# A cross-attention kernel: two TensorE products placed behind their neighbours

## The chip, the cores and the metric

The kernel runs on one core of a Trainium2 chip. A core has TensorE (PE: matrix products, with its weight loads shown apart as PEld), VectorE (DVE), ScalarE (ACT), GpSimd (POOL) and SyncE (SP), and 16 DMA engines. The metric is the time of one execution on the device, in microseconds (us). All data are float32.

## The reference

Thirty-two batches b, each with x and y of 256 channels x 1024 positions:

```python
x_q = einsum('oc,bcn->bno', w_qk, y)
x_k = einsum('oc,bcn->bon', w_qk, x)
x_v = einsum('oc,bcn->bon', w_v, x) + b_v
energy = einsum('bnc,bcm->bnm', x_q, x_k)
attention = softmax(energy, axis=-1)
attention = attention / (1e-07 + attention.sum(axis=1, keepdims=True))
x_r = einsum('bcn,bnm->bcm', x_v, attention)
x_r = relu(einsum('oc,bcn->bon', w_t, x - x_r) + b_t)
return x + x_r
```

So each batch has an energy of 1024 x 1024, a softmax over its rows, a division by its column sums, and a product with the values, followed by a projection, a Relu and a residual.

## The kernel before, in words

**Algebra.** The two uses of `w_qk` are folded into one 256 x 256 matrix, so that a batch has a product "keys" (class `Keys`, tiles `gx`), and the energy is a product of these with y. The value weights and the last projection are folded as well (class `Values`, tiles `ut`), so that the projected result is one accumulation of an x term and an attention term.

**Seven products.** Each of the four matrix products of a batch (keys, values, energy, attention) is cut into 2 x 2 blocks and made from seven products instead of eight, called p1 to p7, in the manner of Strassen and Winograd. They need sums of blocks of both operands (`xs`, `ys`, `gt`, `us`, `et`), and sums of the seven products give the four output blocks (methods `c11`, `c12`, `c21`, `c22`). The seven products of one instance share three PSUM banks of 128 x 512: `one` takes P1, then P6 is added onto it, then P7, then P4; `two` takes P5, then P3 is added; `three` takes P2. Between the additions, ScalarE copies the bank's state to SBUF: `p1s` behind P1, `w` behind P6, `p5s` behind P5. So P6 may not be added to `one` before `p1s` is copied, P7 not before `w`, P3 not before `p5s`, and P4 not before c22 has read `one`. In the profile a copy's name has the class's letter in front: `op5s` is the copy of P5 in the attention (o), `ew` the copy of P6 in the energy (e). PSUM tiles are `po`, `pe`, `pg`, `pu`.

**Energy.** Rows are taken in four pairs t = 0 to 3 (loop at L603), an `Energy` object each. A product of a pair is one 128 x 128 weight block and 512 columns, which TensorE runs as two passes. Combining the blocks on VectorE also finds the row's minimum or maximum for the softmax (rows with `nm`). P4 of a pair is run in the next pair (L632), between that pair's P6 and P3.

**Attention.** One `Attention` object a batch. Each of its products has an x part (`xpart`, L461: one product with the projection weights, two passes) and an e part (`epart`, L466: four row tiles, eight passes). The e operands are the normalised attention and mixes of it that VectorE makes: `et` has t1, t2 and t4. `run` is one hand-written order of all engines' work. While a batch's attention runs, the values of the next batch are finished (`u.p4()` is one of its products, eight passes of 128 columns). The attention's last product P4 (`end()`) and its last output block (`before.c21()`) are done in the next batch's first pair.

**Order.** Every engine but SP is wrapped in `InOrder` (L66): an instruction may not be issued before the one that the program wrote before it on that engine. The order in the text is thus the order on the engine. Most instructions are therefore recorded at L77. DMAs: x, y and the sums' raw blocks are loaded on SP (L95, L236, L237), sums are added by accumulating DMAs issued on POOL (L110), and outputs are stored on SP (L483).

The places of the change: in `run`, the lines L515 to L520; in the main loop, L610 to L628.

Of the kernel before, what the change touches and what calls it, by code (L numbers as in the profile page):

```python
# [16 lines left out]
def kernel(  # L17
# [30 lines left out]
    B, C, N = x.shape  # L48
# [40 lines left out]
    def load(tag, b, pieces=1):  # L89
        from_, p = (x, xp) if tag == "x" else (y, yp)  # L90
        to = p.tile([P, KC, N], F32, tag=tag, name=f"{tag}_{b}")
        from_ = from_[b].rearrange("(k p) n -> p k n", p=P)
        W = KC // pieces
        for j in range(pieces):
            nc.sync.dma_start(to[:, ts(j, W)], from_[:, ts(j, W)])  # L95
        loaded[tag, b] = to
# [121 lines left out]
    def summed(tag, b):  # L218


        p = up if tag == "x" else one
        s = p.tile([P, 4, MB], F32, tag=f"{tag}s", name=f"{tag}s_{b}")
        t1, t3, t4, t2 = (s[:, j] for j in range(4))
        to = loaded[tag, b]
        b11, b12 = to[:, 0, ts(0, MB)], to[:, 0, ts(1, MB)]
        b21, b22 = to[:, 1, ts(0, MB)], to[:, 1, ts(1, MB)]
        if b == 0:
            pool.tensor_tensor(t1, b11, b12, ALU.add)
            pool.tensor_tensor(t2, b22, t1, ALU.add)
            pool.tensor_tensor(t3, b12, b22, ALU.add)  # L230
            pool.tensor_tensor(t4, b21, t2, ALU.add)
            steps = []
        else:
            from_ = (x if tag == "x" else y)[b]
            q = quarters(from_)
            nc.sync.dma_start(s[:, :2], q[:, 0, 1:2, :].to_broadcast([P, 2, MB]))  # L236
            nc.sync.dma_start(s[:, 2:], q[:, 1])  # L237
            steps = [
                lambda: accumulate(s[:, :2], corners(from_)),
                lambda: accumulate(s[:, 2:], s[:, 0:1].to_broadcast([P, 2, MB])),  # L240
                lambda: accumulate(t4, q[:, 1, 1]),
            ]
        return (b11, b21, b22, t4, t1, t2, t3), steps
# [191 lines left out]
    class Attention(Seven):  # L435
# [69 lines left out]
        def run(self, u):  # L505

            self.normal(0, 0)
            if u:
                u.c22()
            self.normal(1, 0)  # L510
            self.normal(0, 1)
            self.mix(self.t1, self.b11, self.b12, ALU.add)
            self.normal(1, 1)
            self.mix(self.t2, self.t1, self.b22, ALU.subtract)
            self.epart(self.one, 1)  # L515
            self.p1s = self.biased(self.one, "p1s", bt[:, 0, :])
            self.epart(self.three, 2)
            self.xpart(self.one, 6, True)
            self.epart(self.two, 5)
            self.p5s = self.biased(self.two, "p5s", bt[:, 1, :])  # L520
            if u:
                u.p4()
                u.c21()
                u.c11()
                u.c12()
            self.c11()
            self.xpart(self.two, 3, True)
            self.epart(self.two, 3, range(HT // 2))
            self.epart(self.one, 6)
            self.w = self.biased(self.one, "w", nbt[:, 0, :])  # L530
            self.mix(self.t3, self.b12, self.b22, ALU.subtract)
            self.mix(self.t4, self.b21, self.t2, ALU.subtract)
            self.epart(self.two, 3, range(HT // 2, HT))
            self.c12()
            self.xpart(self.one, 7, True)
            self.epart(self.one, 7)
            self.c22()
# [5 lines left out]
    def columns(b):  # L543

        part = one.tile([P, NB], F32, tag="part", name=f"part_{b}")
        dve.tensor_reduce(
            part, acc.rearrange("p (j r) -> p j r", r=G32), AX.X, ALU.add, apply_transpose=True
        )
        return part

    def inverse(b, part):

        pS = bank(f"pS_{b}")
        pe.matmul(pS[:, :NB], fold.rearrange("p a c -> p (a c)"), part, start=True, stop=True)
        sc = one.tile([P, NB, 1], F32, tag="sc", name=f"sc_{b}")
        dve.tensor_scalar(sc[:, :, 0], pS[:, :NB], EPS, None, ALU.add)
        dve.reciprocal(sc[:, :, 0], sc[:, :, 0])
        rc = one.tile([P, NB, G32], F32, tag="rc", name=f"rc_{b}")
        dve.transpose(rc.rearrange("p j r -> p (j r)"), sc.to_broadcast([P, NB, G32]))
        return rc.rearrange("p j r -> p (j r)")  # L560
# [37 lines left out]
    before = None  # L598
    for b in range(B):
        more = b + 1 < B  # L600
        pair = []

        for t in range(HT):  # L603
            now = Energy(b, t, lhs, rhs)
            pair.append(now)
            now.p1()
            if t > 0:
                pair[t - 1].exp(1)
            now.p5()
            if t == 0:  # L610
                if before is not None:
                    before.end()
                e = ep.tile([P, NT, N], F32, tag="e", name=f"e_{b}")
                acc = one.tile([P, N], F32, tag="acc", name=f"acc_{b}")
                ur, usteps = u.factors()
            if t > 1:
                pair[t - 2].share(0)
            now.p2()
            now.c11()
            if t == 0 and before is not None:  # L620
                before.c21()
                if b + 1 < B:
                    load("x", b + 1)
            if t == 1:
                pair[0].scale(1)
            if t > 1:
                pair[t - 1].share(1)
            now.p6()  # L628
            if t == 1:
                act.activation(acc, e[:, HT, :], AF.Copy, scale=scales[HT])  # L630
            if t > 0:
                pair[t - 1].p4()  # L632
                pair[t - 1].c21()
                pair[t - 1].exp(0)
            now.p3()
            now.c12()
            now.p7()
            now.c22()
            if t == 0:
                for step in usteps:  # L640
                    step()
                if more:
                    xn, xsteps = summed("x", b + 1)
            elif more:
                xsteps[t - 1]()
        last = pair[-1]

        if more:
            g = Keys(b + 1, xn)
            g.p1()  # L650
        last.exp(1)
        if more:
            g.p5()
        pair[2].share(0)
        last.p4()
        last.c21()
        last.share(1)
        if more:
            load("y", b + 1)
            rhs, ysteps = summed("y", b + 1)  # L660
            g.p6()
        last.exp(0)
        if more:
            g.p2()
            g.c11()
            g.p3()
        last.share(0)
        part = columns(b)
        if more:
            g.p7()  # L670
            g.c12()
            g.c22()
            un = Values(b + 1, xn)
            un.p1()
            un.p5()
            un.p2()
            un.p6()
        else:
            now = Attention(b, xr, ur)
            now.begin()  # L680
        rc = inverse(b, part)
        if more:
            un.p3()
            g.p4()
            g.c21()
            un.p7()
            lhs, gsteps = g.factors()

        if more:
            now = Attention(b, xr, ur)  # L690
            now.begin()
            ysteps[0]()
            now.run(un)
            ysteps[1]()
            un.bias()
            for step in gsteps:
                step()
            ysteps[2]()
            before = now
            xr, u = xn, un  # L700
        else:
            now.run(None)
            now.end()
            now.c21()
# [30 lines left out]
```

## Time and profile before

| What | Value |
|---|---|
| median of three runs | 2175.99 us (2175.93 to 2176.82) |
| the profiled execution | 2176.29 us |
| its span, from the first to the last instruction | 2174.5 us |
| mean granted TensorE clock | 0.997 |
| VectorE busy | 83% |
| ScalarE busy | 36% |
| GpSimd busy | 27% |
| HBM traffic over the span | 99 GB/s |
| one 512-wide pass of TensorE, start to start (16 passes `po<-e,ut` from 470.84 to 477.71) | 0.429 us |
| one batch, from the attention's first pass to the next batch's (468.43 to 535.27 in the chain of waits) | 66.84 us |

The profile is one execution, in which the hardware profiler notes each instruction's start and end. A line of its time line gives start, length, engine, source line, operation, output<-inputs, shapes and count; in square brackets stand the idle time of the engine before it and what ended that. Consecutive instructions of a kind are merged, and the length is then from the first start to the last end. Ends of matmuls are modelled: a matmul's row overlaps the next one, so the distance between starts says more than the length. The chain of waits follows the work back from the last instruction, at each step to what released it, and gives each piece's start and length.

TensorE's waits that the profile shows as idle time are few: 4.5 us at the first batch's end for the DMA `xs<-xs`, 2.7 twice in the last batch, and some below 1.5 us.

### The profile page before, as it was taken

How to read it: one execution, taken by the hardware profiler on the slowest of the kernel's cores; microseconds unless marked ns; L12 is line 12 of the kernel's file. 1: busy time of each engine (PE TensorE's matmuls, PEld its weight loads, DVE VectorE, ACT ScalarE, POOL GpSimd, SP SyncE). 2: the span in 40 equal slices, each digit the busy share in tenths (PEclk: the TensorE clock that was granted, in tenths of full speed). 3: DMA queues.
4: the chain of work that ended last, by engine and by line, in shares of the span. 5: the costliest groups of instructions: out<-in, count | busy, mean ns of one | idle time of the engine just before them, and what ended most of it. 6: DMA issues, size and time to landing. Idle time of an engine off the chain costs nothing.

```text
span 2174.5 us, 19911 instructions
## 1 busy us (share of the span) xinstructions
PE 2154.4 (99%) x6366; PEld 1065.1 (49%) x6366; DVE 1803.9 (83%) x2963; ACT 788.3 (36%) x1321; POOL 597.9 (27%) x488
## 2 busy tenths in 40 slices
PE   8999999999999999999999999999999999999997
PEld 4455445554445545455544555444554545554453
DVE  5798888888888988889888889888898888988887
ACT  4234432344432344333443224443234433344421
POOL 4322323222233223232232322223322323223220
PEclk9999999999999999999999999999999999999999
DMA  5555666556655556565566654665555566546630
GB/s 149 128 115 131 152 139 140 117 120 150 151 126 123 122 142 145 126 147 109 131 155 141 135 121 119 149 149 121 129 123 140 145 127 149 111 126 155 145 74 20
DMA packets 139049, 282.60 MB, mean 130 GB/s; under 512 B 9152, under 2 KB 42688, under 8 KB 138944
## 3 DMA queue, kind: packets, MB, share of 16 engines
q0 software_dynamic: 75936, 114.83, 33.9%
q1 hardware_dynamic: 62464, 166.48, 21.4%
q8 instruction: 51, 0.84, 0.2%
q14 instruction: 54, 0.44, 0.1%
q10 hardware_dynamic: 544, 0.00, 0.0%
HBM read 181.67 MB, written 33.55 MB: 99 GB/s over the span
## 4 chain that ended last, share of the span: by engine, by line
PE 97%; DVE 1%; DMA 1%; POOL 0%; issue 0%; ACT 0%; DVEq 0%
PE po L77 44%; PE pe L77 34%; PE pu L77 9%; PE pg L77 9%; DVE e L77 1%; DMA ut<-uc 0%; DMA xs<-xs 0%; DMA xs<-in_x_dram 0%; POOL us L77 0%; DVE acc L77 0%; PE pS L77 0%; PE idle L142 0%; DVE et L77 0%; PE pw L184 0%; PE pg L169 0%
## 5 line engine op out<-in xcount | busy, mean ns | idle before, releaser
L77 PE MATMUL pe<-gt,ys 128*128 128x512 f32 x768 | 394.9, 596 | 0.0
L77 DVE SCALAR_TENSOR_TENSOR e<-e,ri,rc 128x512 f32<-128x512 f32 x512 | 348.4, 742 | 1.1
L77 DVE SCALAR_TENSOR_TENSOR acc<-e,ri,acc 128x1024 f32<-128x1024 f32 x224 | 287.9, 1285 | 8.0
L77 DVE CUSTOM_DVE_ANT_0 e<-pe,ep1s 128x512 f32<-128x512 f32 x128 | 88.5, 691 | 230.2 <-PE pe L77 161.8
L77 PE MATMUL pe<-gx,y 128*128 128x512 f32 x512 | 261.4, 592 | 0.0
L77 PEld LDWEIGHTS pe<-gt,ys 128*128 128x128 f32 x768 | 143.3, 190 | 189.0 <-issue 168.1
L77 PE MATMUL po<-e,us 128*128 128x512 f32 x512 | 235.4, 592 | 0.0
L77 POOL TENSOR_TENSOR gt<-gx 128x512 f32<-128x512 f32 x64 | 101.7, 1589 | 478.4 <-DVE gx L77 478.4
L77 PE MATMUL po<-et,us 128*128 128x512 f32 x512 | 230.2, 592 | 0.0
L77 PE MATMUL po<-e,ut 128*128 128x512 f32 x512 | 226.9, 596 | 2.7 <-DVE e L77 2.7
L77 ACT ACTIVATE e<-e,nm 128x1024 f32<-128x1024 f32 x128 | 147.1, 1149 | 97.6 <-DVE nm L77 96.2
L77 DVE TENSOR_TENSOR e<-e 128x1024 f32<-128x1024 f32 x64 | 178.9, 2833 | 0.0
L77 ACT COPY ep1s<-pe 128x512 f32<-128x512 f32 x128 | 75.0, 586 | 281.5 <-PE pe L77 277.0
L77 PEld LDWEIGHTS po<-e,ut 128*128 128x128 f32 x512 | 98.0, 192 | 126.0 <-issue 94.8
L77 PEld LDWEIGHTS po<-et,us 128*128 128x128 f32 x512 | 97.3, 190 | 122.5 <-issue 121.5
L77 PEld LDWEIGHTS po<-e,us 128*128 128x128 f32 x512 | 97.3, 190 | 122.5 <-issue 115.3
L77 PEld LDWEIGHTS pe<-gx,y 128*128 128x128 f32 x512 | 97.2, 190 | 122.0 <-issue 121.5
L77 ACT ACTIVATE e<-e,bias 128x1024 f32<-128x1024 f32 x128 | 147.4, 1152 | 0.6 <-DVE ri L77 0.5
L77 POOL DMA_DIRECT2D ut<-uc x32 | 50.7, 1584 | 314.2 <-DVE ut L77 259.0
L77 PE MATMUL pe<-gx,ys 128*128 128x512 f32 x256 | 130.8, 592 | 1.1 <-DVE nm L77 1.1
L77 PE MATMUL pe<-gt,y 128*128 128x512 f32 x256 | 130.7, 592 | 0.0
L77 POOL TENSOR_TENSOR us<-ut 128x512 f32<-128x512 f32 x64 | 82.1, 1283 | 165.0 <-PE po L77 147.8
(113 smaller groups left out, 3303.4 us busy)
## 6 DMA issues: line engine op xcount, KB each, us to landing
y<-in_ctx_dram SPq DMA_DIRECT2D x32, 1024.0 KB, 4.9
ut<-uc POOLq DMA_DIRECT2D x32, 1024.0 KB, 9.7
out_dram<-z SPq DMA_DIRECT2D x128, 256.0 KB, 2.1
x<-in_x_dram SPq DMA_DIRECT2D x31, 1024.0 KB, 7.6
xs<-in_x_dram SPq DMA_DIRECT2D x62, 512.0 KB, 4.5
ys<-in_ctx_dram SPq DMA_DIRECT2D x62, 512.0 KB, 4.2
xs<-in_x_dram POOLq DMA_DIRECT2D x31, 512.0 KB, 6.8
xs<-xs POOLq DMA_DIRECT2D x31, 512.0 KB, 5.0
```

The costliest lines, as they stand in the source:

```text
L77: self.last = getattr(self.engine, name)(*args, **kwargs)
```

## The change

Two products change their places in TensorE's order. In the attention, the x part of P6 is issued behind P5's e part and its copy rather than ahead of P5's e part. In the first energy pair of a batch (t = 0), P6 is issued ahead of P2. To keep the program's order consistent with that, the last output block of the batch before (`before.c21()`) and the load of x for the next batch are written ahead of these two products as well. In pairs 1 to 3 the order stays. What is computed stays the same.

```diff
             self.p1s = self.biased(self.one, "p1s", bt[:, 0, :])
             self.epart(self.three, 2)
-            self.xpart(self.one, 6, True)
             self.epart(self.two, 5)
             self.p5s = self.biased(self.two, "p5s", bt[:, 1, :])
+            self.xpart(self.one, 6, True)
             if u:
                 u.p4()
                 u.c21()
...
             if t == 0:
                 if before is not None:
                     before.end()
+                    before.c21()
+                    if more:
+                        load("x", b + 1)
...
             if t > 1:
                 pair[t - 2].share(0)
+            if t == 0:
+                now.p6()
             now.p2()
             now.c11()
-            if t == 0 and before is not None:
-                before.c21()
-                if b + 1 < B:
-                    load("x", b + 1)
             if t == 1:
                 pair[0].scale(1)
             if t > 1:
                 pair[t - 1].share(1)
-            now.p6()
+            if t > 0:
+                now.p6()
```

In TensorE's order, the attention goes from "P1 e, P2 e, P6 x, P5 e, u.p4, P3 x" to "P1 e, P2 e, P5 e, P6 x, u.p4, P3 x". The first pair goes from "P1, P5, end(), P2, P6, P3, P7" to "P1, P5, end(), P6, P2, P3, P7". On VectorE the last addition of `before.c21()` comes ahead of c11 of the first pair. ScalarE's, GpSimd's and SP's orders are the same as before.

## The prediction

> **What bounds the kernel now.** I read the page's busy shares first, then the chain of waits, then the time lines around the two places that the diff touches. The page:
>
> ```profile
> PE 2154.4 (99%) x6366; PEld 1065.1 (49%) x6366; DVE 1803.9 (83%) x2963; ACT 788.3 (36%) x1321; POOL 597.9 (27%) x488
> ```
>
> TensorE is busy nearly all the time, so most of its time is work that this change keeps. Only its waits can be saved, and most of these are too short to stand as idle time: the busy row of a matmul that started late is simply longer. So I count distances between starts. Sixteen passes `po<-e,ut` run from 470.84 to 477.71, which is 0.4294 us a pass; a 512-wide product is two passes, 0.86 us. A product of the values is eight 128-wide passes: 528.67 to 529.56, 0.89 us. Now the chain of one batch (start, length, engine, tile, count):
>
> ```profile
> 535.27 13.73 PE po L77 x32
> 549.01 0.89 PE pu L77 x8
> 549.90 12.22 PE po L77 x28
> ...
> 568.13 21.54 PE pe L77 x50
> ```
>
> All of it is TensorE. 32 passes take what they should (13.74). But 28 passes should take 12.02 and take 12.22, and 50 should take 21.47 and take 21.54. A batch (66.85 us) thus loses about 0.2 us behind `u.p4` and 0.07 in the energy. The time line of the first place:
>
> ```profile
> 549.10 0.69 ACT L77 ACTIVATE op5s<-po,bt 128x512 f32<-128x512 f32 x1 [7.03 <-PE po L77]
> 549.84 0.30 PEld L77 LDWEIGHTS po<-x,wtTs 128*128 128x128 f32 x2
> 549.84 1.12 PE L77 MATMUL po<-x,wtTs 128*128 128x512 f32 x2
> ```
>
> ScalarE's copy of P5 ends at 549.79; the x part of P3, which adds onto the same bank, loads its weights 0.05 us later, and its two loads stand together, so the first pass begins at 549.94. `u.p4` had ended its eight passes at 548.85 + 0.89 = 549.74. Loss 0.20 us. The second place, in the first energy pair:
>
> ```profile
> 502.84 1.02 PE L77 MATMUL pe<-gt,y 128*128 128x512 f32 x2
> 503.04 0.59 ACT L77 COPY ew<-pe 128x512 f32<-128x512 f32 x1 [1.03 <-PE pe L77]
> 503.67 0.30 PEld L77 LDWEIGHTS pe<-gt,ys 128*128 128x128 f32 x2 [0.65 <-ACT ew L77]
> 503.70 1.10 PE L77 MATMUL pe<-gt,ys 128*128 128x512 f32 x2
> 504.64 1.02 PE L77 MATMUL pe<-gx,y 128*128 128x512 f32 x2
> ```
>
> Row 1 is P3, row 4 P7, which adds onto the bank that `ew` copies. 502.84 to 504.64 is 1.80 us where two products take 1.72: loss 0.08 us. In later pairs P4 of the pair before stands between P6 and P3, so the copy is hidden.
>
> **The change part by part.** No instruction is added or removed; a few stand elsewhere.
>
> *P6's x part behind P5.* It moves from before P5's four e tiles to behind them, so P5 and its copy end 0.86 us earlier while `u.p4` and the x part of P3 keep their places. The copy would end at 549.79 - 0.86 = 548.93; the x part of P3 wants its weights at about 549.63. The wait goes: 0.20 us in batches 0 to 30. The moved x part itself waits for `op1s`, which begins at 541.38 and takes 0.69: long done. In batch 25 the same distance holds 0.28 us more (the row at 1753.35 shows 0.21 idle for `op5s`); that goes too. In the last batch there is no `u.p4` between:
>
> ```profile
> 2147.76 3.60 PE L77 MATMUL po<-et,us 128*128 128x512 f32 x8
> 2152.14 1.13 PE L77 MATMUL po<-x,wtTs 128*128 128x512 f32 x2 [0.78 <-ACT op5s L77]
> 2153.10 1.88 PE L77 MATMUL po<-e,us 128*128 128x512 f32 x4
> ```
>
> From 2147.76 eight passes and a product would end at 2152.05, not 2153.10: loss 1.05. With 0.86 us of other work put in between, 0.19 remains: gain 0.86. What follows there isn't bound by VectorE (it idles 1.90 and 2.82 us before its next outputs), so the gain arrives at the end. Part sum: 30 x 0.20 + 0.48 + 0.86 = 7.3 us.
>
> *The cover that is lost.* P5's e tiles now begin 0.86 us earlier, and their operand is t1, which VectorE has only just made:
>
> ```profile
> 543.09 2.34 DVE L77 TENSOR_TENSOR et<-e 128x1024 f32<-128x1024 f32 x2
> ...
> 544.55 1.02 PE L77 MATMUL po<-xs,wtTs 128*128 128x512 f32 x2
> ```
>
> Each half of t1 takes 1.21 us (group mean 1211 ns). Half one is ready at 544.30 and P5 now wants to begin at 544.55: 0.25 us. Half two is ready at 545.43 for a pass at 546.27: far enough. How long from VectorE's end to the first pass? The two waits above give 0.05 to the load and 0.10 more to the pass, 0.15. But P5's first tile waits for two engines (t1 from VectorE, `us` from POOL), and its t1 wait stands as an own instruction in TensorE's queue. The nearest row for that is `pg<-xs,gs` in the opening: `gs` ends at 8.59 (8.30 + 0.29), the loads come at 8.70, the first pass at 8.81: 0.22 us. Ends: 0.15 gives no wait; half as much again as 0.22, 0.33, would be late by 0.08. I take 0.22, the same kind of wait: no stall, but only 0.03 us to spare. The far end gives back 31 x 0.08 = 2.5 us. All that TensorE has to do stands behind this wait, so nothing else would fill it.
>
> *P6 ahead of P2 in pair 0.* P6 now begins at 501.12, where P2 stood. What it waits for is old by then: `ep1s`, the copy of its own bank (496.21 + 0.59), and a sum of y that POOL's `ys<-ys` makes. That is issued once a batch, 27 us before (540.83 for the P6 near 568), and the like transfer `xs<-xs` lands 5.0 us after issue. `ew` comes at 502.18 instead of 503.04, behind the Relu of `c21` on ScalarE (501.32 + 0.69 = 502.01), and ends at 502.77; P7 wants its weights at 503.27. The wait goes: 0.08 us. In batch 0 it buys nothing, since TensorE then stands 4.55 us for the DMA `xs<-xs`. 31 x 0.08 = 2.5 us. P2 is 0.86 us later, and its c11 on VectorE with it: from 502.29 to 503.15, done by 503.84, and VectorE's next (c12) begins at 504.00. The last addition of `before.c21`, which stood behind c11, now goes ahead of it, at about 502.05; what is queued behind it is c11, which comes later anyway. So the store and the load of x on SP leave about 0.85 us earlier (503.62 and 504.01 before); no transfer stands behind them until `y` at 522.00, and x is first used at 522.66. POOL's order is unchanged; its `xs<-in_x_dram` waits for a landing from SP's earlier transfers, which keep their place ahead of that store.
>
> *What is late next.* With TensorE 0.20 us earlier from `u.p4` on, it meets VectorE at the x part of P4: c22 frees that bank at 495.31 + 0.69 = 496.00, VectorE having been free at 495.21. Weights are wanted at 496.40, now 496.20. It holds, with 0.2 us.
>
> Sum: 7.3 + 2.5 = 9.8; unrounded distances (0.201 and 0.083) make it 9.9 us. The profiled execution took 2176.29 us with a span of 2174.5. 2176.29 - 9.9 = **2166.4 us**, 0.45% less. The median shown, 2175.99, is 0.3 lower, about batch 25's slip, so from it the same figure follows.
>
> **A rule against the change.** The row first: a mix of VectorE (`e<-e`, two SBUF inputs) has a mean of 2833 ns where `et<-e` has 1211; at 552.79 one half takes 4.73 us with POOL's two `gt` operations beside it. The Trainium skill's page "SBUF — State Buffer", section "SBUF: two separate sides", says that VectorE with two SBUF inputs and GpSimd reading SBUF take one port pair in turns, whole instructions at a time. t1 is such a mix, and it is now needed 0.86 us sooner. POOL's `ys<-ys` issue runs from 540.83 to 542.04, 1.05 us ahead of t1 (a program's jitter takes it nearer in some batches: waiting on a DMA, it isn't tied to VectorE). Were an issue also such a holder, t1 could be held for its 1.21 us, and the sum would turn. The trace says otherwise: eight normalising products (also two SBUF inputs) beside it take 5.38 us, 0.67 each, against 2.72 for four at 545.36 with no POOL work, 0.68. I take the row: cost nothing.
>
> **The rivals.**
> 1. *t1 shows.* The two-engine wait takes 0.27 to 0.33 us, or VectorE's t1 is a little later: 0.02 to 0.08 us a batch come back. Time 2167 to 2169. For it: 0.03 us to spare. Against: the same kind of wait measured 0.22.
> 2. *VectorE paces the attention.* It is busy almost without a break from 534.48 to 564; if TensorE cannot run ahead of it, the 0.20 us returns as a wait at P4's x part. Left: the second move and the last batch, 2.5 + 0.9: 2172.9. Against: 0.2 us of room there, and VectorE's chain starts from TensorE's own `pS`.
> 3. *Slower: POOL meets t1.* `ys<-ys` falls onto t1 and holds it. By its own length t1's half one is 1.21 us late; 0.03 is spare, so 1.18 a batch is lost against 0.28 won: 31 x 0.90, less the last batch's 0.9: about 2203. It decides from a t1 that is 0.31 us later than now. For it: the rule, and a mix that was held 3.3 us elsewhere. Against: nothing in the change moves POOL towards t1, and the row beside it shows no hold.
> That the moves don't happen is excluded: the engines' orders are written out by hand and the built program has them.
>
> **How the numbers follow.** Forecast 0.76, rival 1 0.12, rival 2 0.06, rival 3 and other losses 0.06. The forecast's own spread is what the runs before show (0.9 us) and the few half-speed passes in the first and last batch, whose place may shift: 2165.0 to 2167.5. To leave no more than 2 in 10 out with rival 1 taken in: 2165.0 to 2169.2. A change within 0.2% (4.4 us) can't be told from none; rival 2 (3.4 us) lies there. Faster 0.88, same 0.06, slower 0.06.
>
> **What would show it.** Right: in the time line of one batch the x part of P3 follows `u.p4` by 0.89 us; pair 0's P3 and P7 take 1.72; a batch is 66.57 us; P5's first pass follows the last `e,ut` pass by 0.43. Wrong: paired loads of `po<-et,us` with an idle before them for `et` (rival 1); loads of `po<-xs,wtT` waiting for `z` (rival 2); `et<-e` above 1.21 us (rival 3); or an `op5s` or `ew` wait that stays.

## The result, and the profile after

| | before | changed |
|---|---|---|
| median of six runs each | 2176.77 us (2175.93 to 2179.37) | 2169.29 us (2167.93 to 2170.11) |
| ratio of the two, 95% interval | | 0.9962 (0.995 to 0.9975) |
| profiled execution | 2176.29 us, span 2174.5 | 2169.38 us, span 2167.6 |

The change is faster by 7.5 us of the medians, 0.34%, and the interval of the ratio lies clear of 1. The forecast was 2166.4 us, 9.9 us less than the profiled execution; the range reached to 2169.2, and the median lies 0.1 above it.

The page's first row, after the change:

```profile
PE 2147.3 (99%) x6366; PEld 1064.3 (49%) x6366; DVE 1806.0 (83%) x2963; ACT 787.7 (36%) x1321; POOL 597.3 (28%) x488
```

7.1 us less of TensorE's busy time, with the same instructions: what went is the stretch in started matmuls, not work. Next the chain of waits of the changed kernel (start, length, engine, tile, count), one batch:

```profile
469.11 13.73 PE po L77 x32
...
501.77 21.46 PE pe L77 x50
...
535.67 13.73 PE po L77 x32
```

From the first line to the last is one batch: 66.56 us, where the forecast said 66.57 and before had 66.85. The 50 passes of the energy, 21.54 before, take 21.46; 50 times 0.4294 gives 21.47. The time line at the first move:

```profile
543.49 2.35 DVE L77 TENSOR_TENSOR et<-e 128x1024 f32<-128x1024 f32 x2
...
544.10 0.19 PEld L77 LDWEIGHTS po<-e,ut 128*128 128x128 f32 x1 [0.24 <-issue]
544.82 0.32 PEld L77 LDWEIGHTS po<-et,us 128*128 128x128 f32 x2 [0.53 <-issue]
544.96 1.45 PE L77 MATMUL po<-et,us 128*128 128x512 f32 x3
...
549.25 1.05 PE L77 MATMUL pu<-wvtT,xs 128*128 128x128 f32 x8
...
550.14 1.02 PE L77 MATMUL po<-x,wtTs 128*128 128x512 f32 x2
```

Two things are to be seen. The x part of P3 follows `u.p4` by 0.89 us, the eight passes and nothing more: the wait for P5's copy is gone. And the first weights of P5, usually loaded a whole pass (0.43 us) ahead, come 0.72 us behind the load before them, 0.14 ahead of their pass, and 0.12 behind the end of t1's half one (543.49 + 1.21 = 544.70). So the loads did wait there for t1, but within the pass that was running. The time line at the second move:

```profile
501.60 1.02 PE L77 MATMUL pe<-gt,ys 128*128 128x512 f32 x2
...
502.66 0.58 ACT L77 COPY ew<-pe 128x512 f32<-128x512 f32 x1 [0.17 <-PE pe L77]
...
503.32 1.02 PE L77 MATMUL pe<-gt,y 128*128 128x512 f32 x2
...
504.18 1.02 PE L77 MATMUL pe<-gt,ys 128*128 128x512 f32 x2
...
505.04 1.02 PE L77 MATMUL pe<-gx,y 128*128 128x512 f32 x2
```

P6, the copy `ew`, P3, P7 and the next pair's P1: P3 to P1 is 1.72 us, and the copy ends 0.94 us before P7 begins.

So the batches gained what was forecast. That includes batch 25, whose pS to pS is 0.28 us longer than the others in the kernel before and like the others in the changed one. I cut both spans at the small matmul `pS`, of which each batch has one:

| stretch | before | changed | difference | forecast |
|---|---|---|---|---|
| up to the first pS | 64.32 | 66.72 | +2.40 | 0 |
| 30 batches, pS to pS | 2005.66 | 1996.80 | -8.87 | -8.8 |
| the last one, pS to pS | 64.86 | 64.57 | -0.29 | -0.3 |
| behind the last pS | 39.67 | 39.51 | -0.15 | -0.9 |
| span | 2174.51 | 2167.61 | -6.91 | -9.9 |

The missing 3 us are all at the two ends; the end is taken up below, with the account of the prediction. At the front it is the first batch's stall. The time line of the kernel before, with SP's queue (SPq), POOL and TensorE:

```profile
47.64 0.37 SPq L95 DMA_DIRECT2D y<-in_ctx_dram  x1
...
48.85 1.20 POOL L77 DMA_DIRECT2D xs<-xs  x1 [5.34 <-DMA xs<-in_x_dram]
...
55.54 0.67 PE L77 MATMUL pg<-xs,gs 128*128 128x512 f32 x1 [4.55 <-DMA xs<-xs]
```

and after the change:

```profile
48.21 1.20 POOL L77 DMA_DIRECT2D xs<-xs  x1 [4.95 <-DMA xs<-in_x_dram]
...
48.59 0.37 SPq L95 DMA_DIRECT2D y<-in_ctx_dram  x1
...
58.01 2.05 PE L77 MATMUL pg<-xs,gs 128*128 128x512 f32 x2 [5.68 <-DMA xs<-xs]
```

The transfer `xs<-xs` is a link in a chain of three accumulating DMAs that make the sums of x for batch 1. Before, it was issued behind the load of y and let TensorE go on 6.7 us after; in the changed kernel it was issued 0.4 us ahead of that load and took 9.8. Is that the change, or does it differ from execution to execution? That was the first question for the experiments.

### The profile page after: what moved, and what is told of

It reads as the page before. It is cut to its first block, busy times and chain, and to the rows that moved or that the text cites. A ratio compares the mean times of both kernels' runs of the same rounds, so it can differ in the third digit from the quotient of the medians.

```text
span 2167.6 us, 19880 instructions
## 1 busy us (share of the span) xinstructions
PE 2147.3 (99%) x6366; PEld 1064.3 (49%) x6366; DVE 1806.0 (83%) x2963; ACT 787.7 (36%) x1321; POOL 597.3 (28%) x488
## 4 chain that ended last, share of the span: by engine, by line
PE 98%; DMA 1%; DVE 1%; issue 0%; POOL 0%; ACT 0%; DVEq 0%
PE po L77 44%; PE pe L77 34%; PE pu L77 9%; PE pg L77 9%; DMA xs<-xs 0%; DMA ut<-uc 0%; DMA xs<-in_x_dram 0%; PE idle L142 0%; DVE acc L77 0%; PE pS L77 0%; POOL us L77 0%; DVE e L77 0%; PE pw L184 0%; PE pg L169 0%; DVE z L77 0%
## 5 line engine op out<-in xcount | busy, mean ns | idle before, releaser
L77 DVE TENSOR_TENSOR z<-z,x 128x512 f32<-128x512 f32 x32 | 22.1, 692 | 153.9 <-ACT z L77 153.9
```

The lines of the kernel that those rows point to most:

```text
L77: self.last = getattr(self.engine, name)(*args, **kwargs)
```

## The experiments

**Theory:** each batch gains the 0.20 and 0.083 us of the two waits and nothing else of the change costs anything; what is short of the forecast lies in the first batch and the tail, and differs between executions whatever the kernel. **Rivals:** the change costs some 2 us of its own; VectorE paces the attention, so that the first wait only moves.

**Four kernels with the first batch's stall taken out.** In batch 0 the three DMAs go ahead of the sums `us` on POOL, which wait until 35 us for another transfer. This edit is on all four; on top of it comes none of the change, all, or one of its moves.

```diff
-            if t == 0:
+            if b == 0:
+                if t == 0:
+                    xn, xsteps = summed("x", 1)
+                if t < 3:
+                    xsteps[t]()
+                else:
+                    for step in usteps:
+                        step()
+            elif t == 0:
                 for step in usteps:
                     step()
                 if more:
```

*Neither move:*

> The kernel before with another order on POOL in the first batch alone: the three accumulating DMAs that make the sums of x for batch 1 go ahead of the four sums us, which need a transfer that lands only at 35 us. Theory (the first batch's DMA chain is one link of sums after another, bound by what stands ahead of it on POOL): TensorE's wait for xs<-xs (4.55 us in the profile before) and the half-speed stretch behind it (4.35 us where three products take 2.58, so 1.8) vanish: 6.3 us less than before, about 2170, ratio 0.997. Rival (the wait comes from the loads of y that share the DMA engines with it): the wait stays at 4 us or more, and the time stays within 2 us of before.

*Both moves:*

> The changed kernel with that same order in the first batch. Theory (the steady batch gives 0.286 us and nothing else of the change costs anything; the 2 us that the measured gain is short of the forecast are the first batch's stall, which differs from run to run): 31 x 0.286 + 0.86 + 0.08 = 9.8 us less than first_none, about 2160, ratio to before 0.9926. Rival (the change itself costs some 2 us at the first batch or the end): 7.5 to 8 us less than first_none, about 2162.

*The first alone:*

> The first move alone (P6's x part behind P5 in the attention), with the first batch's new order. Theory of the waits: 31 x 0.20 + 0.86 = 7.1 us less than first_none, about 2163. Rival (VectorE paces the attention, so that the wait only moves to the x part of P4): 0.9 us less than first_none, about 2169.

*The second alone:*

> The second move alone (P6 ahead of P2 in pair 0), with the first batch's new order. Theory of the waits: 32 x 0.083 = 2.7 us less than first_none, about 2167.4; together with first_attn it gives first_both's gain. Rival (the earlier load of x and the later c11 cost something): less than 1.5 us.

Measured beside the kernel before (median 2178.27 us here), five rounds:

| kernel | median, us | ratio to before (95%) | against first_none | one batch, pS to pS |
|---|---|---|---|---|
| first_none | 2171.32 | 0.9968 (0.9956 to 0.9981) | | 66.845 |
| first_attn | 2164.62 | 0.9939 (0.9926 to 0.9953) | -6.70 | 66.644 |
| first_energy | 2168.36 | 0.9954 (0.9942 to 0.9967) | -2.96 | 66.761 |
| first_both | 2161.74 | 0.9925 (0.9912 to 0.9937) | -9.58 | 66.560 |

TensorE's wait for `xs<-xs` is gone in all four (first pS at 58.0 to 59.0 us), as the theory of the POOL chain said. Its rival, that the loads of y make the wait, is not refuted by that: the loads of y are where they were, but `xs<-xs` now runs well ahead of them. The time line of first_none, POOL and SP's queue:

```profile
39.77 1.19 POOL L77 DMA_DIRECT2D xs<-xs  x1 [10.02 <-DMA xs<-in_x_dram]
45.07 0.90 POOL L77 DMA_DIRECT2D xs<-in_x_dram  x1 [4.10 <-DMA xs<-xs]
...
48.34 0.37 SPq L95 DMA_DIRECT2D y<-in_ctx_dram  x1
```

With no load of y beside it, `xs<-xs` lands 5.0 us after its issue, as its median over all batches does, and the next link of the chain goes 5.3 us after it. In the profile of before the next link took 6.9 us (48.85 to 55.70), in that of the changed kernel 9.9 (48.21 to 58.16). The place in the chain and the neighbouring transfers thus both have a part in the stall.

The two moves together give 9.58 us, 0.2 short of the 9.8 expected and clear of the rival's 7.5 to 8; the first alone gives 6.70 where 7.1 was expected, the second 2.96 where 2.7 was. That the sum comes so close is in part luck: by the two profiles it is 9.2 us, with 0.4 gained ahead of the first pS and less than forecast in the first batch and behind the last pS. What stands firm is the batch: it gains 0.201 by the first move, 0.084 by the second, 0.285 by both. VectorE does not pace the attention. first_both is also the fastest version of all: 16.5 us below before.

A part of the first batch in it went the way of the prediction's rival 1. The time line of first_both, VectorE and TensorE at batch 0's attention:

```profile
70.07 2.34 DVE L77 TENSOR_TENSOR et<-e 128x1024 f32<-128x1024 f32 x2
71.39 0.30 PEld L77 LDWEIGHTS po<-et,us 128*128 128x128 f32 x2 [1.61 <-issue]
71.42 1.10 PE L77 MATMUL po<-et,us 128*128 128x512 f32 x2 [0.81 <-DVE et L77]
```

Here t1 is late, and P5 waits for it: that batch (pS to pS) takes 67.61 us, 1.05 more than the others, and in first_none, where P6's x part still stands between, only 0.31 more. The lost cover thus costs 0.74 us once. t1 starts 11.9 us behind pS there and 10.85 in the other batches, and VectorE works without a break in between. Two things hold it up. It still has work in hand when pS is done, and takes up the result 0.81 us after pS began instead of 0.35: an accumulation `acc<-e,ri,acc` that usually takes 1.28 us took 2.21 at 50.30 (50.83 in first_none), beside POOL's `us` sums, now at 45 to 52 us. And the first normalising product takes 1.43 us instead of the 0.80 of a later batch, beside POOL's `gt<-gt,gx`.

**Both kernels as they are, once more.**

> The changed kernel as it is, once more. Theory (the steady batch is 66.56 us each time; what differs between executions is the first batch's stall for xs<-xs and the half-speed stretches at the start and the end): batches of 66.56 again, a total between 2166 and 2170, and the difference from the profile of the changed kernel lies ahead of the first pS. Rival (the change costs 2 us of its own): the first pS again near 66.7 us, as in that profile, where before had 64.3.

> The kernel before as it is, once more, for its profile. Theory: batches of 66.85 us; the first pS anywhere from 63 to 68 us, so that 64.3 in its first profile was one draw. Rival: the first pS at 64.3 again within 0.5 us.

after_again: median 2169.69 us of five, before 2178.05 beside it, ratio 0.9963 (0.9949 to 0.9976). Its batch is 66.560 us again, its first pS at 66.89. before_again: 2178.30 us in one execution, batch 66.847, the first pS at 66.55. So before's own first pS moved by 2.2 us between two profiles, as the theory asked: its first profile had the short stall, the other the long one. Of the six profiles of kernels that kept that stall (these, the first two and the two below), five issued `xs<-xs` 0.2 to 0.4 us ahead of the load of y and had TensorE go on 9.3 to 10.1 us later; only before's first profile had it behind the load, and 6.7 us. What set the order can be read earlier in the traces. The kernel before, VectorE and POOL, in its first profile and then in before_again:

```profile
39.94 1.28 DVE L77 SCALAR_TENSOR_TENSOR acc<-e,ri,acc 128x1024 f32<-128x1024 f32 x1
39.99 2.36 POOL L77 TENSOR_TENSOR us<-ut,us 128x512 f32<-128x512 f32 x1
```

```profile
40.72 2.38 DVE L77 SCALAR_TENSOR_TENSOR acc<-e,ri,acc 128x1024 f32<-128x1024 f32 x1
40.76 1.27 POOL L77 TENSOR_TENSOR us<-ut,us 128x512 f32<-128x512 f32 x1
```

The accumulation and POOL's last `us` sum start within 0.06 us of each other, and one of the two takes 1.1 us longer than alone. In before's first profile it is POOL's sum, and the DMAs that POOL issues behind it come later: `xs<-xs` 13.6 us behind the first `us` sum, where it is 12.2 to 12.4 in the other five profiles, in which the accumulation is the longer one. The load of y keeps its place to 0.2 us (12.4 to 12.6). So the same kernel can go either way, though one profile alone has the short form. Whether the change makes the long form likelier was not settled: of the changed kernel's eleven runs the lowest took 2167.93 us, not 2166.4, and of 25 runs of the kernel before five lie below 2177, but only a profile shows which form a run had.

**Double the missing cover.** In t1_early, P5's first tile is asked for one tile sooner:

```diff
-            self.epart(self.three, 2)
-            self.epart(self.two, 5)
+            self.epart(self.three, 2, range(HT - 1))
+            self.epart(self.two, 5, range(1))
+            self.epart(self.three, 2, range(HT - 1, HT))
+            self.epart(self.two, 5, range(1, HT))
```

> The changed kernel with P5's first e tile put ahead of P2's last, so that TensorE asks for t1 0.86 us earlier still. It measures the wait that the prediction put at 0.22 us from VectorE's end to the first pass, with 0.03 us to spare. By 0.22 the pass is 0.86 - 0.03 = 0.83 us late in batches 0 to 30: 25.7 us more than the changed kernel, about 2195. By 0.15 (a wait for one engine) it is 0.76 late: 23.6 more. By 0.33 it is 0.94 late: 29 more.

Measured: 2195.03 us, ratio to before 1.0078 (1.0065 to 1.0092); 25.3 us above after_again. One batch is 67.388 us, 0.828 above 66.560. In its time line, VectorE's t1 and what follows it on TensorE:

```profile
548.38 2.35 DVE L77 TENSOR_TENSOR et<-e 128x1024 f32<-128x1024 f32 x2
549.71 0.30 PEld L77 LDWEIGHTS po<-et,us 128*128 128x128 f32 x2 [1.39 <-issue]
549.74 1.10 PE L77 MATMUL po<-et,us 128*128 128x512 f32 x2 [0.59 <-DVE et L77]
...
550.67 0.59 PE L77 MATMUL po<-e,ut 128*128 128x512 f32 x1
```

Half one ends at 548.38 + 1.21 = 549.59, and the loads come 0.12 us later. The next row starts at 550.67, two passes of 0.43 behind the first one, which thus began at 549.81: 0.22 us. The 0.22 of the prediction holds, so the changed kernel does run with 0.03 us to spare.

**Take the other cover away.** In no_cover, the kernel before has `u.p4` behind the x part of P3:

```diff
+            self.xpart(self.two, 3, True)
             if u:
                 u.p4()
                 u.c21()
                 u.c11()
                 u.c12()
             self.c11()
-            self.xpart(self.two, 3, True)
```

> The kernel before with the eight passes of u.p4 moved from ahead of the x part of P3 to behind it, so that nothing hides P5's copy. Theory (the x part of P3 waits for op5s, and what stands between hides it one for one): the wait grows from 0.20 to the 1.05 us of the last batch, 31 x 0.85 = 26.4 us more, about 2203, ratio 1.012. Rival (VectorE paces the attention; the wait only shows where TensorE has time): less than 10 us more.

Measured: 2206.84 us, ratio 1.0133 (1.0119 to 1.0147); one batch 67.740, which is 0.894 above before where 0.85 was expected. Its time line, ScalarE and TensorE:

```profile
490.06 0.69 ACT L77 ACTIVATE op5s<-po,bt 128x512 f32<-128x512 f32 x1 [7.03 <-PE po L77]
490.81 1.13 PE L77 MATMUL po<-x,wtTs 128*128 128x512 f32 x2 [0.83 <-ACT op5s L77]
```

The wait is there in full and follows `op5s` by 0.06 us. The copy's wait is hidden one for one by what stands between: `u.p4` takes 0.89 us, and without it a batch is 0.894 longer. The 0.85 of the expectation came from the last batch, where `op5s` starts 0.63 us behind P5's last pass instead of the 0.68 here; why it does stays open.

## Why the prediction was right, and where its size was off

- *The first move, 0.20 us a batch:* right. 0.201 by first_attn, and no_cover shows the same wait with nothing to hide it.
- *The second move, 0.08 us a batch:* right, 0.084 by first_energy. The earlier load of x and the later c11 cost nothing that shows: P3 and P7 follow each other without a gap, and the batch has the whole gain.
- *The lost cover of t1:* right, with 0.22 taken and 0.22 measured. Rival 1, "t1 shows", did not happen in the batches of the changed kernel. It did happen in batch 0 of first_both, where VectorE was late for another reason, and by 0.08 us in the last batch of after_again, where P5's eight passes take 3.51 us (2139.92 to 2143.43) instead of 3.43.
- *What is late next:* the x part of P4 did not meet VectorE; a batch keeps its whole 0.286. Rival 2 falls.
- *The rule against the change:* t1 stays at 1.21 us (1.206 to 1.220 in all batches), so rival 3 did not happen. That an issue would not hold it is less well shown: in the changed kernel's profile `ys<-ys` ends at least 0.35 us ahead of t1 in every batch, so the two did not meet, and the row with the normalising products beside such an issue remains the evidence. But the rule of the Trainium skill's page "SBUF — State Buffer", section "SBUF: two separate sides", agrees with the trace elsewhere: the accumulation has two SBUF inputs and stands beside POOL's sums, which read SBUF, and either it takes 2.2 to 2.4 us instead of 1.28 or POOL's sum takes 2.36 instead of 1.27.
- *The sum:* too large, by 2.4 us of the medians and 3.0 of the profiles. The waits were sized right; what was mis-sized are the two ends of the span. First, the first batch, for which the sum has nothing. It was read from one execution, which had the short stall of 4.55 us; the changed kernel's profile had the long one, and its first pS came 2.40 us later. The kernel before, run again beside the experiments, has medians of 2178.05 and 2178.27 us, not 2175.99. Set against these the change gives 8.4 us (after_again), and with the stall out of the way 9.6. Second, the 0.86 us of the last batch. The time lines of TensorE behind the last pS (which starts at 2134.84 before and at 2128.09 after), before and after the change:

```profile
2138.03 9.04 PE L77 MATMUL po<-e,ut 128*128 128x512 f32 x16 [2.74 <-DVE e L77]
2146.90 1.02 PE L77 MATMUL po<-xs,wtTs 128*128 128x512 f32 x2
```

```profile
2131.24 9.79 PE L77 MATMUL po<-e,ut 128*128 128x512 f32 x16 [2.74 <-DVE e L77]
2140.86 3.60 PE L77 MATMUL po<-et,us 128*128 128x512 f32 x8
```

  The gain itself is there: behind the 16 passes, before needs 27.61 us to the end of its span (2146.90 to 2174.51) and the changed kernel 26.75 (2140.86 to 2167.61), 0.86 less. But the 16 passes took 8.87 us before and 9.62 after, at mean granted clocks of 0.78 and 0.72. Both profiles have one stretch of half clock here, of 6.8 us. Before, it begins at 2135.07, 0.2 us behind pS, so that the first 3 us of it fall into TensorE's wait for VectorE and cost nothing; after, it begins at 2129.78, 1.7 us behind pS, and 1.5 us more of it fall on passes. That took 0.75 back. In after_again the stretch is 3.4 us long, and the 16 passes take 8.52. So this part differs between executions of one kernel, like the stall.
- *The range:* the forecast's own spread, "what the runs before show (0.9 us)", was too small: three runs had shown 0.9, six showed 3.4. The prediction named the half-speed passes whose place may shift, but allowed about 1 us either way for all of it. That the median still falls at the edge of the range is luck: its upper end was set for rival 1, which did not happen.
- *Batch 25:* the 0.28 us did go. But they are no slip of one execution: before_again and first_none have the same longer batch (67.126 and 67.125 us), so it isn't why the median lay 0.3 below the profiled execution. What is longer there is the start of `op5s`, 0.96 us behind P5's last pass instead of 0.68, in the changed kernel too, where it is covered.

## What to carry to other kernels

A busy engine can still be waiting: where 99% busy leaves no idle rows, count distances from start to start and compare them with the pitch of the same instruction elsewhere. A wait for a copy is paid off by placing independent work of the right length between the two uses of a bank, but the work that leaves its old place uncovers what stood behind it, so the margin there has to be worked out to the same hundredths. A gain summed over a steady loop can be read to 0.001 us a turn, while the total carries what differs between executions at the start and the end; compare the loop, and take the stall at the start out before judging a few microseconds.

## What the runs showed of the hardware that was not expected

- The same accumulating transfer `xs<-xs` released TensorE 6.7 us after its issue when the load of y was issued 1.2 us ahead of it, and 9.3 to 10.1 us after when it was issued 0.2 to 0.4 us ahead of that load. With no load beside it, in first_none, it landed in 5.0. Why being first is slower stays open.
- Which of two instructions of VectorE and POOL was held, for 1.1 us, went with hundredths of a microsecond: with the accumulation recorded 0.06 us ahead it was POOL's sum, with 0.03 to 0.04 us ahead it was the accumulation (six profiles).
- Around TensorE's stall in batch 0 the trace's record of the granted clock has it at half for 3.4 us in before's first profile (4.55 us idle) and for 6.8 us in the other five (5.4 to 5.9 us idle); in the last batch it is 6.8 us, but 3.4 in after_again. The Trainium skill's page "TensorE: Matmul & The Clock Gate", Part 1, section "What's actually happening", states a window of about 3.4 us that runs freely; these lengths agree with one and two of it, and the place of the stretch in the last batch differs from profile to profile, from 0.5 us ahead of the last pS to 2.6 behind it.
- From the end of t1 to P5's first pass, with `us` to wait for on the same matmul, it took 0.22 us in t1_early; from the end of `op5s` to the first pass that waits for it alone 0.15 to 0.16. That the second engine makes the difference is argued from the program, not shown.
